# A cross-attention and mixture-of-experts block on one core: four differences moved, two PSUM banks read by other engines, one broadcast in two halves

## The chip, the cores and the metric

The kernel runs on one core of a Trainium2 chip. The metric is the device time of one execution in microseconds (us). Before the change it was 457.9 us, the median of three runs (457.46 to 458.61).

The engines are named as the profile names them: PE (TensorE, matrix products, with PEld for the loading of its stationary operand), DVE (VectorE), ACT (ScalarE), POOL (GpSimd) and SP (the queue that issues most transfers). Each engine works through its own list of instructions in order.

## The reference

Eight sequences of 512 tokens with 256 features (x) each have a context of 64 rows and a condition vector. All is float32.

```python
nx = layer_norm(x, ln_gamma, ln_beta)                    # (8, 512, 256)
k, v = context @ Wk, context @ Wv                        # (8, 64, 256)
scores = einsum('bth,bph->btp', nx @ Wq, k) * 256 ** -0.5
evidence = softmax(scores) @ v
combined = concatenate([nx, evidence, anchor], axis=-1)  # 768 features
router_probs = softmax(combined @ router_W + router_b)   # 3 experts
h = silu(einsum('btc,ecr->bter', combined, e_w1) + e_b1) # 512 features per expert
expert_out = einsum('bter,erh->bteh', h, e_w2) + e_b2
routed = sum(expert_out * router_probs[..., None], axis=-2)
g = sigmoid(silu(combined @ gate_w1 + gate_b1) @ gate_w2 + gate_b2)
return x + g * (routed @ out_w + out_b)
```

Two rearrangements matter below. The evidence times the middle rows of an expert's first weight is computed as softmax(scores) times (v W), so that the kernel needs the products of v and W once for each sequence. And the router's probabilities weigh h ahead of the second layer, so that each row of h is multiplied by a number that belongs to the token and the expert.

## The kernel before

**Pairs.** The eight sequences are worked on in four pairs, j = 0 to 3. A pair goes through three stages: `gate_layer` (first layer of the gate), `half_layers` (first layers of the three experts, a table of slots that fixes the order of products and of the steps of the other engines) and `outputs` (second layers, gate, and the results' way out). Much of what pair j + 1 needs ahead of its gate layer is put into `outputs` of pair j, at points with names: "begin", "gate", "P1", "P8", "P5", "P6", "P2", "P7", "P3", "P4", in this order. The dictionaries `between` and `within` hold what is run at each point of `outputs` and of `gate_layer`. The whole body stands under a schedule written out by hand: each engine executes its instructions in the order in which the program issues them.

**Products of two sequences at once.** Blocks are multiplied by a scheme with seven products in place of eight (as Strassen's): sums and differences of blocks go in, and three banks of PSUM, called u, y and z, gather the results, so that a bank is read in the middle of a sequence of products, and the next product adds to what it holds. A product that comes after such a read has to wait for the engine that reads.

**The late products.** For the last two pairs (j = 2 and 3, `JS` is 2) the products of v and W are made by this scheme too, in two parts: part 0 holds the columns of the first two experts (512 columns to a product), part 1 those of the third expert (256 columns). `block_columns` names the blocks of W and where their differences go: in part 0 t1 lies in `ow_sb`, t2 in `mr` and t4 in a tile of its own; in part 1 t1 and t2 lie in the two halves of `ow_sb` and t4 in `mr`. `late_difference(part, n)`, n = 0 to 3, makes one of the four differences on DVE (line L885 of the profile). `late_product(part, n, ps)` makes product n, and `late_values` returns four steps, `first` to `fourth`, with the products and the reads of the banks between them: ACT copies (`nc.scalar.copy`, lines L911, L917, L923 and L928) and DVE additions (`plus`, L906).

Part 0 is run inside `outputs` of pair 1: `first` at "P5", `second` and `third` at "P6", to either side of the scores, `fourth` at "P7". The step that `third` returns, the DVE addition, is run after the exponents (`late.pop()()`). Part 1 is run inside `gate_layer` of pair 2: after the products 1, 5, 6 and 7 of the gate. There `third` and its addition are run together. The four differences that part 1 reads, `late_difference(1, n)`, are issued at "P3" of pair 1's `outputs`, after the third expert sum (`finish`, lines L1431 to L1433 on DVE and L1434 on POOL) and ahead of `turn_weights` (L743, L745).

`fourth` starts with product 4 into u, followed by product 3 into z.

**The router's weights.** `spread_probabilities` stores the probabilities of a pair, transposed, into a small tile `pd` in DRAM (four rows: two sequences times two halves of the tokens; four transfers, L800) and loads it, spread over all 128 partitions, into `pb` (one transfer, L804). Both are issued from POOL's queue. `weigh_chunk` (L1022) multiplies h by the part of `pb` that belongs to its sequence (`S["pb", j][:, i, ...]`), and `bias_sum` (L1406, L1411) reads it too. The order of these multiplications on DVE follows the slots' tables; in pair 0 it begins with three of the first sequence (i = 0), then one of the second; in the later pairs with one of the first, then additions, then one of the second.

Each transfer has a semaphore, and the engines that read its tile wait for it.

Of the kernel before, what the change touches and what calls it, by code (L numbers as in the profile page):

```python
# [16 lines left out]
def kernel(  # L17
# [51 lines left out]
    nc = tc.nc  # L69
    P = 128  # L70
# [29 lines left out]
    def bank(i, name):  # L100
        ps = psum.tile([P, 512], F32, tag=f"b{i}", name=name)
        bank_of[ps.name] = i
        return ps

    def spares(*banks):
        spare[:] = banks
# [469 lines left out]
    S = {}  # L576
# [216 lines left out]
    def spread_probabilities(j):  # L793

        n = E * NJ
        prT = work.tile([P, TB], F32, tag="prT", name=f"prT_{j}", bufs=1)
        nc.vector.transpose(prT, pr)
        pd = dram.tile([len(SIDES), E * NH], F32, tag="pd", name=f"pd_{j}")
        for q, (i, h) in enumerate(SIDES):
            nc.gpsimd.dma_start(  # L800
                pd[q].rearrange("(n c) -> n c", c=TB), prT[q * TB : q * TB + n, :]
            )
        S["pb", j] = work.tile([P, 2, 2, E, NH], F32, tag="pb", name=f"pb_{j}", bufs=1)
        nc.gpsimd.dma_start(  # L804
            S["pb", j].rearrange("p i h e t -> p (i h) (e t)"), pd.partition_broadcast(P)
        )

    def by_side(flat):
        return flat.rearrange("p (h t) -> p h t", h=2)
# [51 lines left out]
    def block_columns(part):  # L861

        if part not in late_v:
            if part == 0:
                c0, n = 0, RH
                t4 = const.tile([P, RH], F32, tag="late_t4", name="late_t4")
                ts = ow_sb.rearrange("p k n -> p (k n)"), mr[:, :, : B // 2, :], t4
            else:
                c0, n = 2 * RH, RH // 2
                ts = ow_sb[:, 0, :], ow_sb[:, 1, :], mr[:, 0, : B // 2, :].rearrange("p b c -> p (b c)")  # L870
            w = [
                [w1[:, KH + k, c0 + i * n : c0 + (i + 1) * n] for i in range(2)] for k in range(KH)
            ]
            late_v[part] = w, ts
        return late_v[part]

    def like(a, b):
        return a.rearrange("p (k n) -> p k n", k=KH) if len(b.shape) > 2 else a
# [9 lines left out]
    def late_product(part, n, ps, start=False):  # L888

        ((b11, b12), (b21, b22)), ts = block_columns(part)  # L890
        t1, t2, t4 = (t.rearrange("p k b c -> p k (b c)") if len(t.shape) > 3 else t for t in ts)
        rhs = {1: b11, 2: b21, 3: b22, 4: t4, 5: t1, 6: t2, 7: b12}[n]
        product(like(ps, rhs), block_rows(n), rhs, start)

    def late_homes(part):
        (c0, n) = (0, RH) if part == 0 else (2 * RH, RH // 2)
        first, second = S["vw", JS], w1[:, KH, :]
        return [a[:, c0 + i * n : c0 + (i + 1) * n] for a in (first, second) for i in range(2)]

    def late_values(part, banks):  # L900

        n = RH if part == 0 else RH // 2
        u, y, z = (bank(i, f"ps_late_{m}")[:, :n] for i, m in zip(banks, "uyz"))

        def plus(dst, ps):
            nc.vector.tensor_tensor(dst, dst, ps, ALU.add)  # L906

        def first():
            c11 = late_homes(part)[0]
            late_product(part, 1, u, True)  # L910
            nc.scalar.copy(c11, u)  # L911
            late_product(part, 2, y, True)
            plus(c11, y)

        def second():
            late_product(part, 6, u)
            nc.scalar.copy(late_homes(part)[1], u)  # L917

        def third():
            c22 = late_homes(part)[3]  # L920
            late_product(part, 7, u)
            late_product(part, 5, z, True)
            nc.scalar.copy(c22, z)  # L923
            return lambda: plus(c22, u)

        def fourth():
            late_product(part, 4, u)
            nc.scalar.copy(late_homes(part)[2], u)  # L928
            late_product(part, 3, z)
            plus(late_homes(part)[1], z)  # L930
            for g in (0, 1) if part == 0 else (2,):
                value_differences(JS, g)

        return first, second, third, fourth

    GROUPS = (NE // 2, *range(NE // 2))
# [4 lines left out]
    def product(ps, lhsT, rhs, start=False):  # L941

        return nc.tensor.matmul(ps, lhsT, rhs, start=start, stop=True, skip_group_check=not start)  # L943
# [587 lines left out]
    with tc.manual_schedule(engines=None):  # L1531
# [85 lines left out]
        for j in range(NP):  # L1617


            within, between = {}, {}  # L1620

            def put(where, n, step, *args):
                where.setdefault(n, []).append(lambda: step(*args))

            spares(7, 5)
            if j == 0:
                spares(4, 5, 1)
                copies = []

                def value_product(g):  # L1630
                    value_weights(0, g, lambda *args: copies.append(args), False)

                def copy_values():
                    nc.scalar.copy(*copies.pop(0))

                put(within, 1, value_product, 0)
                put(within, 1, begin_softmax)
                put(within, 5, copy_values)
                put(within, 6, load_table, AF.Silu)
                put(within, 3, value_product, 1)  # L1640
                put(within, 3, copy_values)
                put(within, "sums", end_softmax)
                put(within, 7, value_product, 2)
                put(within, 7, copy_values)
                put(within, 7, end_setup)
            elif j < JS:
                put(within, 3, value_weights, j, 1, nc.scalar.copy, False)
            elif j == JS:
                first, second, third, fourth = late_values(1, (6, 5, 7))
                put(within, 1, first)  # L1650
                put(within, 5, second)
                put(within, 6, lambda third=third: third()())
                put(within, 7, fourth)
            if j + 1 < NP:
                b0, b1 = 2 * j + 2, 2 * j + 3
                if j + 2 < NP:
                    put(between, "begin", load_x, b0 + 2)
                    put(between, "begin", load_x, b1 + 2)
                put(between, "begin", transpose_blocks, b0)
                put(between, "gate", regroup_x, b1)  # L1660
                put(between, "begin", value_weights, j + 1, E)
                put(between, "begin", store_router_rows, j + 1)
                put(between, "begin", spread_router_rows, j + 1)
                put(between, "P8", transpose_blocks, b1)
                if j + 1 == JS:
                    put(between, "P6", lambda: late[1]())
                put(between, "P6", scores, j + 1)
                if j + 1 == JS:
                    put(between, "P6", lambda: late.append(late[2]()))
                put(between, "P6", exponents, j + 1)  # L1670
                if j + 1 == JS:
                    put(between, "P6", lambda: late.pop()())
                put(between, "P6", combine_x, j + 1, nc.gpsimd)
                if j + 1 < JS:
                    put(between, "P6", value_weights, j + 1, 2)
                elif j + 1 == JS:

                    def late_start():
                        late[:] = late_values(0, (0, 2, 4))

                    put(between, "P1", late_start)
                    put(between, "P5", lambda: late[0]())
                    for n in range(4):
                        put(between, "P3", late_difference, 1, n)
                put(between, "P7", softmax, j + 1)
                if j + 1 < JS:
                    put(between, "P7", value_weights, j + 1, 0)
                elif j + 1 > JS:
                    put(between, "P7", value_differences, j + 1, 0)
                    put(between, "P3", value_differences, j + 1, 1)  # L1690
                put(between, "P7", evidence_logits, j + 1)
                put(between, "P7", router_logits, j + 1)
                if j + 1 == JS:
                    put(between, "P7", lambda: late[3]())
                put(between, "P3", turn_weights, j + 1)
                put(between, "P3", router_exp, j + 1)
            gate_layer(j, within)
            half_layers(j)
            outputs(j, between)
# [34 lines left out]
```

## Time and profile before

| | |
|---|---|
| median of the runs | 457.9 us |
| time of the profiled execution | 458.82 us |
| its span | 456.8 us |
| PE busy | 450.8 us, 1,801 matmuls |
| DVE busy | 363.6 us, 698 instructions |
| ACT busy | 214.5 us, 378 instructions |
| POOL busy | 95.2 us, 153 instructions |
| chain of waits, by engine | PE 87%, DVE 6%, DMA 3% |
| pb: KB each, issues | 1,536 KB, 4 |
| pb: from issue to landing | 6.5 to 8.3 us, median 7.2 |
| DVE idle until pb has landed | 6.6 us in two waits, the longer 5.1 |

The profile is of one execution. Its span runs from the first to the last instruction on the engines; the execution's own time is 2.0 us longer. A matmul's record is longer than its share of the engine, since matmuls are pipelined: a row of the timeline with "x2" and 1.02 us is two matmuls of 512 columns, and the next one starts 0.86 us after the first. So whether PE stands still is read from the starts of its matmuls. A weight load (PEld) is issued ahead of its matmul, and part of its wait is hidden. In rows of a timeline the columns are the start and the duration in us, the engine, the line, the operation, the tiles written and read, and in brackets the time that the engine was idle before and what ended it.

Four pairs mean four passes with nearly the same rows: pair 0 to about 100 us (its first part holds the set-up, its end the preparation of the second layers), pair 1 from there to 250, pair 2 to 355, pair 3 to the end, each `outputs` with the next pair's preparation in it.

### The profile page before, as it was taken

To read this page: it belongs to the slowest core of one execution; us is meant where nothing else is said; L and a number is where in the kernel's file an instruction comes from. 1 tells how busy PE (TensorE), PEld (TensorE's weight loads), DVE (VectorE), ACT (ScalarE), POOL (GpSimd) and SP (SyncE) were. 2 spreads that over 40 slices of the span, in tenths; PEclk is the share of its full clock that TensorE was granted. 3 is DMA by queue.
4 is the path that set the end of the run, shared out by engine and by line. 5 is a ranking of instruction groups with operands and counts; after the bars stand their busy time and mean duration, and the time that the engine had idled before them with its cause. 6 is when DMAs were issued, how large, how long until landed. Compare 5 with 4: busy or idle time off the path is not lost.

```text
span 456.8 us, 5532 instructions
## 1 busy us (share of the span) xinstructions
PE 450.8 (99%) x1801; PEld 220.0 (48%) x1801; DVE 363.6 (80%) x698; ACT 214.5 (47%) x378; POOL 95.2 (21%) x153
## 2 busy tenths in 40 slices
PE   9999999999999999999999999999999999999996
PEld 7554445664444444444444444444444445654445
DVE  2878989949698799769769999767979937677983
ACT  2545864564501675466240377558430356558000
POOL 5466600252431200001431220000252310000010
PEclk9999999999999999999999999999999999999999
DMA  8984672364012377202002238401202282000004
GB/s 263 384 174 103 101 242 37 59 126 51 3 23 47 88 197 137 65 0 47 7 11 35 43 144 165 67 0 19 35 0 47 41 201 36 1 0 0 1 17 76
DMA packets 119380, 35.32 MB, mean 77 GB/s; under 512 B 106012, under 2 KB 116312, under 8 KB 118840
## 3 DMA queue, kind: packets, MB, share of 16 engines
q1 hardware_dynamic: 115344, 27.02, 28.9%
q0 software_dynamic: 2080, 7.16, 4.6%
q10 hardware_dynamic: 1928, 0.80, 0.6%
q8 instruction: 14, 0.23, 0.2%
q14 instruction: 14, 0.11, 0.1%
HBM read 27.56 MB, written 7.39 MB: 77 GB/s over the span
## 4 chain that ended last, share of the span: by engine, by line
PE 87%; DVE 6%; DMA 3%; POOL 1%; issue 1%; ACT 0%; ACTq 0%; DVEq 0%; POOLq 0%
PE ps_u L943 39%; PE ps_z L943 18%; PE ps_y L943 13%; PE ps_gu L943 3%; PE ps_vw L822 3%; PE ps_w2o L547 2%; DMA pb<-pd 2%; PE ps_s L691 2%; PE ps_gz L943 2%; PE ps_tokens L943 1%; DVE h L1401 1%; DMA scr_w<-in_L_xcond_Wk_dram 1%; PE ps_v L356 1%; PE ps_late_u L943 1%; PE ps_m L356 1%; PE ps_gy L943 1%
## 5 line engine op out<-in xcount | busy, mean ns | idle before, releaser
L943 PE MATMUL ps_u<-nxT,w 64*128 64x512 f32 (+1 forms) x208 | 96.9, 591 | 0.0
L1022 DVE TENSOR_TENSOR h<-h,pb 128x512 f32<-128x512 f32 x96 | 62.6, 684 | 17.1 <-ACT h L979 10.4
L943 PE MATMUL ps_u<-h,w2o 128*128 128x512 f32 x144 | 63.9, 593 | 0.0
L979 ACT ACTIVATE h<-h,abias 128x512 f32<-128x512 f32 x72 | 49.1, 717 | 31.3 <-DVE h L985 31.2
L943 PE MATMUL ps_y<-nxT,w 64*128 64x512 f32 (+1 forms) x104 | 51.7, 590 | 0.0
L943 PE MATMUL ps_z<-nxT,ws 64*128 64x512 f32 (+1 forms) x104 | 51.5, 591 | 0.0
L943 PE MATMUL ps_z<-T,ws 64*128 64x512 f32 (+1 forms) x104 | 51.5, 590 | 0.0
L943 PEld LDWEIGHTS ps_u<-nxT,w 64*128 64x128 f32 (+1 forms) x208 | 37.4, 187 | 25.4 <-issue 22.1
L943 PE MATMUL ps_u<-T,ws 64*128 64x512 f32 (+1 forms) x104 | 49.4, 590 | 0.0
L943 PE MATMUL ps_u<-T,w 64*128 64x512 f32 x112 | 48.5, 590 | 0.0
L943 PEld LDWEIGHTS ps_u<-h,w2o 128*128 128x128 f32 x144 | 27.3, 190 | 32.9 <-issue 32.3
L943 PE MATMUL ps_z<-h,w2s 128*128 128x512 f32 x96 | 42.5, 592 | 0.0
L943 PE MATMUL ps_z<-wT,vw 64*128 64x512 f32 x78 | 39.2, 590 | 0.0
L988 ACT COPY h<-ps_u 128x512 f32<-128x512 f32 x48 | 27.7, 580 | 21.5 <-PE ps_u L943 21.4
L1434 POOL TENSOR_TENSOR yb<-yb,xb 128x512 f32<-128x512 f32 x14 | 20.8, 1483 | 69.9 <-DVE yb L1433 56.8
L1401 DVE TENSOR_TENSOR h<-h,h 128x1024 f32<-128x1024 f32 x24 | 30.9, 1342 | 0.0
L943 PEld LDWEIGHTS ps_z<-h,w2s 128*128 128x128 f32 x96 | 18.2, 190 | 23.0 <-issue 22.0
L943 PEld LDWEIGHTS ps_y<-nxT,w 64*128 64x128 f32 (+1 forms) x104 | 19.4, 187 | 12.2 <-issue 12.2
L943 PEld LDWEIGHTS ps_z<-T,ws 64*128 64x128 f32 (+1 forms) x104 | 19.2, 187 | 12.1 <-issue 10.9
L943 PEld LDWEIGHTS ps_z<-nxT,ws 64*128 64x128 f32 (+1 forms) x104 | 19.0, 187 | 12.0 <-issue 9.2
L943 PEld LDWEIGHTS ps_u<-T,ws 64*128 64x128 f32 (+1 forms) x104 | 18.3, 187 | 12.8 <-issue 11.9
L943 PEld LDWEIGHTS ps_u<-T,w 64*128 64x128 f32 x112 | 18.6, 187 | 12.2 <-issue 11.5
(271 smaller groups left out, 847.1 us busy)
## 6 DMA issues: line engine op xcount, KB each, us to landing
pb<-pd POOLq DMA_DIRECT2D x4, 1536.0 KB, 7.2
xb<-in_x_dram SPq DMA_DIRECT2D x64, 64.0 KB, 2.4
out_dram<-yb SPq DMA_DIRECT2D x56, 64.0 KB, 1.9
x<-in_x_dram SPq DMA_DIRECT2D x24, 128.0 KB, 2.8
xd<-x SPq DMA_DIRECT2D x24, 128.0 KB, 2.6
xg<-xd SPq DMA_DIRECT2D x48, 64.0 KB, 2.3
w<-in_L_xcond_e_w_dram SPq DMA_DIRECT2D x4, 512.0 KB, 6.9
scr_wa<-in_L_xcond_e_w_dram SPq DMA_DIRECT2D x3, 512.0 KB, 9.4
```

The lines of the kernel that those rows point to most:

```text
L356: nc.tensor.matmul(ps, w_sb[:, k, m * P : (m + 1) * P], src[:, k, :], start=(k == 0), stop=(k == KH - 1))
L547: nc.tensor.matmul(ps[:, d * H : (d + 1) * H], w2["T"][u % 2][:, c : c + P], ow_sb[:, k, :], start=(k == 0), stop=(k == KH - 1),)
L691: nc.tensor.matmul(ps[side(i, h), g * NH : (g + 1) * NH], mr[:, k, 2 * j + i, g * TB : (g + 1) * TB], S["nxT", 2 * j + i][:, k, h * NH : ( ...
L822: nc.tensor.matmul(ps, vT[:, k, j * 2 * CT : (j + 1) * 2 * CT], w1[:, KH + k, n0:n1], start=(k == 0), stop=(k == KH - 1),)
L943: return nc.tensor.matmul(ps, lhsT, rhs, start=start, stop=True, skip_group_check=not start)
L979: nc.scalar.activation(h, h if src is None else src, AF.Silu, bias=abias[:, c, 2 * j + i : 2 * j + i + 1])
L988: nc.scalar.copy(chunk(n, i, d), part)
L1022: nc.vector.tensor_tensor(h, h, S["pb", j][:, i, :, 2 * q // RC, :], ALU.mult)
L1401: nc.vector.tensor_tensor(d, p, m, ALU.subtract)
L1434: nc.gpsimd.tensor_tensor(yb, yb, S["xb", 2 * j + row][:, i, :], ALU.add)
```

## The change

Three places are edited.

1. `spread_probabilities` loads `pb` by two transfers, one for each sequence of the pair (two rows of `pd` each). Each waits for the two stores into its own rows.
2. `third` in `late_values` (used by both parts): ACT copies the bank u right after product 7, and DVE adds the bank z, where ACT copied z after product 5, and DVE added u.
3. The four `late_difference(1, n)` are issued at "P6" of pair 1's `outputs`, behind the addition of part 0's `third`, and no longer at "P3".

```diff
@@ spread_probabilities @@
-        nc.gpsimd.dma_start(
-            S["pb", j].rearrange("p i h e t -> p (i h) (e t)"), pd.partition_broadcast(P)
-        )
+        for i in range(2):
+            nc.gpsimd.dma_start(
+                S["pb", j][:, i].rearrange("p h e t -> p h (e t)"),
+                pd[2 * i : 2 * i + 2].partition_broadcast(P),
+            )
@@ late_values @@
         def third():
             c22 = late_homes(part)[3]
             late_product(part, 7, u)
+            nc.scalar.copy(c22, u)
             late_product(part, 5, z, True)
-            nc.scalar.copy(c22, z)
-            return lambda: plus(c22, u)
+            return lambda: plus(c22, z)
@@ the loop over the pairs @@
                 put(between, "P6", exponents, j + 1)
                 if j + 1 == JS:
                     put(between, "P6", lambda: late.pop()())
+                    for n in range(4):
+                        put(between, "P6", late_difference, 1, n)
                 put(between, "P6", combine_x, j + 1, nc.gpsimd)
...
                     put(between, "P1", late_start)
                     put(between, "P5", lambda: late[0]())
-                    for n in range(4):
-                        put(between, "P3", late_difference, 1, n)
```

In the changed kernel's lists the products on PE, the copies on ACT and the operations on DVE keep their number and, but for the four differences on DVE, their order. What differs is the waits: product 4 of either part waits for ACT where it waited for DVE, product 3 for DVE where it waited for ACT, product 6 of part 1 for ACT alone. POOL issues four transfers more in all.

## The prediction

> **What bounds the kernel now.** First the page: TensorE is busy almost all the time, and its granted clock stands at the top digit in all forty slices.
>
> ```profile
> PE 450.8 (99%) x1801; PEld 220.0 (48%) x1801; DVE 363.6 (80%) x698; ACT 214.5 (47%) x378; POOL 95.2 (21%) x153
> ```
>
> So no edit that leaves the matmuls alone can win more than the stretches in which TensorE stands still, and it wins those only where it moves what TensorE waits for. I therefore read the waits of the weight loads, the chain of waits at the places the diff touches, and then the timeline there. In the waits (who <- whom: total us, times, longest) three groups matter:
>
> ```profile
> PEld ps_u L943 <- DVE h L985: 4.8, 9, 1.2
> ...
> PEld ps_late_u L943 <- DVE w L906: 1.8, 1, 1.8
> PEld ps_late_u L943 <- ACT vw L911: 0.9, 1, 0.9
> ```
>
> A weight load runs ahead of its matmul, so these are not yet stalls. A stall shows in the starts of the matmuls: without one, full 128-column products of 512 columns follow each other every 0.43 us (half that at 256 columns; a 64-row product runs beside its partner, so a pair also takes 0.43). I count what starts late against this pace.
>
> At the start of pair 2 (TensorE, start and us):
>
> ```profile
> 252.32 1.02 PE L943 MATMUL ps_z<-T,ws 128*128 128x512 f32 x2
> 253.40 0.67 PE L943 MATMUL ps_late_u<-ow_sb,vT 128*128 128x256 f32 x2
> ...
> 257.35 1.02 PE L943 MATMUL ps_u<-nxT,w 128*128 128x512 f32 x2
> 259.31 0.70 PE L943 MATMUL ps_late_u<-mr,vT 128*128 128x256 f32 x2 [0.94 <-DVE w L906]
> ```
>
> 252.32 + 2 x 0.43 = 253.18, so the first starts 0.22 us late, and its pair takes 0.08 too long (the restart): 0.30. The second is due at 258.21 and starts at 259.31: 1.10, plus 0.11 of restart: 1.21. VectorE at that time:
>
> ```profile
> 230.15 0.68 DVE L906 TENSOR_TENSOR w<-w,ps_late_u 128x512 f32<-128x512 f32 x1
> 233.63 0.69 DVE L1431 TENSOR_TENSOR r<-r,ps_y 128x512 f32<-128x512 f32 x1 [2.81 <-PE ps_y L943]
> ...
> 251.46 0.38 DVE L885 TENSOR_TENSOR ow_sb<-w 128x256 f32<-128x256 f32 x1
> 251.88 1.38 DVE L885 TENSOR_TENSOR ow_sb<-w,ow_sb 128x256 f32<-128x256 f32 x1
> ...
> 258.85 0.41 DVE L906 TENSOR_TENSOR w<-w,ps_late_u 128x256 f32<-128x256 f32 x1
> ```
>
> It runs without a pause from 233.63 to 259.85. The four differences (L885, 251.46 to 253.85: 2.39 us) lie inside that run, ahead of the addition (258.85 to 259.26) whose end releases the late product at 259.31. Before 233.63 it is idle for 2.81 us.
>
> In pair 0 the chain of waits (start, us) goes through the broadcast of the router's weights:
>
> ```profile
> 56.70 7.84 DMA pb<-pd
> 64.57 2.50 DVE h L1022 x4
> 67.07 0.61 DVE h L985
> 67.72 0.69 PE ps_u L943
> ```
>
> VectorE ends its last step at 63.10 and idles 1.47 us for pb. From 64.57 to 91 it never rests again, and TensorE stalls behind it: at 67.72 (due 67.21) 0.62 with the restart; between 76.41 and 79.55, where six steps take 3.14 instead of 2.57, 0.57; at 80.44, 0.13. Sum 1.32. In pair 3 VectorE idles 5.14 us for pb (371.93 to 377.07); TensorE feels 0.20 of it (378.41, due 378.31, and 0.10 restart). Pairs 1 and 2 have no wait on pb.
>
> Together the diff's places hold 1.32 + 0.20 + 0.30 + 1.21 = 3.03 us of stalled TensorE.
>
> **The differences, and which engine reads which bank.** Added and removed instructions on TensorE, VectorE and ScalarE: none; only order and operands change.
>
> *Part 0 (third() in pair 1, near 227).* ScalarE's copy now follows product 7 (done about 227.5) and not product 5 (its copy started at 228.48), so the copy, the logits copy behind it and the exponentials come about 1 us earlier; VectorE's addition then waits for product 5, done about 228.4, and ends near 229.9 instead of 230.83. TensorE has no stall from 229 to 253, so this wins nothing itself. Then the four differences: their nearest rows are 0.38, 0.41 and 0.41, starting 0.33 to 0.42 apart, so about 1.5 us; at worst the 2.39 of their old place. They end between 231.4 and 232.3 (from 230.83: at most 233.2), ahead of 233.63, in VectorE's idle time: price 0. If that cover were gone, the row-sum chain after 233.63 would start up to 2.4 us later, and be where it is today by 253.85.
>
> *Pair 2.* VectorE's queue is 2.39 us shorter from 251.46 on: the two additions L906 move from 258.54 to about 256.2, the second then waiting for product 5 (done about 256.6), so ending near 257. The product at 253.40 no longer waits for the difference (its bank was read by ScalarE at 252.52): its 0.30 goes. The product at 259.31 now waits for ScalarE's copy of u. That copy was at 256.69 behind product 5; behind product 7 it ends near 256.4. It is due at 257.9: no stall. Product 3, next, waits for VectorE's addition near 257 and is due at 258.3. So 1.51 goes. Margin: 1.3 us.
>
> What could eat it is GpSimd working beside VectorE:
>
> ```profile
> 251.61 1.36 POOL L1434 TENSOR_TENSOR yb<-yb,xb 128x512 f32<-128x512 f32 x1 [7.95 <-DVE yb L1433]
> ```
>
> It covers the difference that took 1.38 instead of 0.41. After the move a transpose (L743) stands there; in pair 3 one ran beside the same GpSimd line (356.40 to 357.91) in 0.71 us, its ordinary 0.71. The Trainium skill (SBUF — State Buffer, "SBUF: two separate sides") says that a VectorE operation with two SBUF inputs and a GpSimd operation exclude each other for a whole instruction. By it the differences could lose up to one GpSimd operation in their new place too, where the last of GpSimd's four (228.60 to 229.87) ends as they begin. Their dearest row, 2.39 us, fits in any case, as shown above. I take 1.51; bounds 0.3 (only the first stall goes) and 1.51.
>
> **The broadcast in two.** One issue (0.56 us on GpSimd) becomes two, eight instead of four in all; GpSimd has nothing urgent behind them (a memset of 0.12). The first half waits for two of the four small stores only. Those are issued 0.5 us apart, so it can go about 1 us earlier (55.7); the second goes at about 56.7 as today. The trace's DMA records show what the 7.84 us hold: nothing until 57.97, then 128 packets of 12,288 bytes over 16 engines, eight each, median 0.545 us, the slowest engine ending at 64.15. Half as many bytes per packet: the first half lands between 60 and 61.5 (four old packets' worth, or the slow engine's half), if time goes by bytes. If it goes by packets, it lands like today's whole less 1 us: 63.5. VectorE wants it at 63.10. The second half is wanted only at 64.9 (three products of 0.6 later); by bytes it is there by 64.6, by packets (2 x 8 x 0.545 from 57.0) at about 66. VectorE is ahead of today until the second half comes later than 64.57 + 1.8 = 66.4.
>
> By bytes VectorE gains 1.47 in pair 0 and keeps it, since the sums it reads next are all finished earlier than that; TensorE's 1.32 goes (upper end 1.55, with a stall of 0.23 at 87.78 that a transpose on VectorE ends). By packets VectorE resumes its fourth product at 66 and not 66.4: some 0.4. Nearest row: packets of 1,024 bytes in the same records take 0.046 to 0.07, so bytes decide; I take 1.32. In pair 3 the half is there before ScalarE's silu (373.72) lets VectorE go: 0.20.
>
> The Trainium skill (DMA: Bandwidth & Descriptors, "Anatomy of one DMA") speaks against the split: about 2 us fixed per DMA and bytes at 436 GB/s. By it two halves one after the other would be an estimated 7.6 us against 5.6 for the whole; from 55.7 that is 63.3 for the second.
>
> **Sum.** 1.51 + 1.32 + 0.20 = 3.03 us. The profiled execution took 458.82 (span 456.8 and 2.0 around it), 0.9 over the median of the runs, 457.9; its stalls count the same in both. 457.9 - 3.0 = **454.9**. Its own range: 454.2 (with the 0.23 and scatter) to 455.8.
>
> **Rivals.**
> - *Only the late products win.* Both halves land together, or packets decide: 457.9 - 1.5 = 456.4. For it: one queue, the same 16 engines. Against: the second half starts behind the first. 0.10.
> - *The wait moves to product 3.* It now needs VectorE's addition, where ScalarE's copy was enough. If VectorE arrives as late as today (259.3), product 3, due 258.3, stalls 1.0: of 1.51 remains 0.5, total 455.9. For it: the addition is still last of a long run. Against: 2.39 us less ahead of it. 0.12.
> - *Nothing shows:* the next late engine takes the stalls back, 457.6 to 457.9. Against: from 264 to 309 no product starts late. 0.07.
> - *Slower: the second half comes late.* If a half-size packet takes as long as a whole one on the slow engine too (6.2 us for eight, so 12.4 for sixteen, from 57.0), it lands at 69.8: 3.4 us past 66.4, and pair 3 likewise (11.7 from 369.1 against 380.07) 1.5. 457.9 - 1.5 + 3.4 + 1.5 = 461.3. It decides from a landing at about 68. Against: the 1,024-byte rows. 0.05.
>
> **How the numbers follow.** All three terms: 0.66. Range 454.0 to 456.8: it takes in the first two rivals and leaves out the last two. About 0.3% (1.4 us) is what a measurement of this kernel can tell from no change, so faster means under 456.5: 0.66 + 0.12 + half of the first rival, less a little for scatter, 0.80. Same: 0.14. Slower: 0.06.
>
> **What would show it.** Right: no wait of ps_late_u on VectorE; L885 near 230; two pb issues per pair, the first landed by 62 in pair 0, and L1022 starting at 63.1. Wrong: VectorE idle before the fourth L1022 of pair 0 past 66.4; a late product 3; the stalls at 78 and 80 still there.

## The result, and the profile after

The changed kernel takes 455.19 us in the median of six runs (454.99 to 455.48), against 457.81 for six runs of the kernel before beside them: a ratio of 0.994 (0.9928 to 0.9953), 2.6 us less. The profiled execution took 454.99 us, its span 453.2.

The page's busy times and the chain of waits by engine:

```profile
PE 448.6 (99%) x1801; PEld 214.4 (47%) x1801; DVE 363.8 (80%) x698; ACT 214.5 (47%) x378; POOL 96.8 (21%) x157
...
PE 99%; DVE 0%; issue 0%
```

The counts are the old ones but for POOL, which has the four further transfers. The chain that was 87% PE, 6% DVE and 3% DMA is now PE alone: for nearly the whole span it never leaves TensorE for another engine.

In the waits of the weight loads (who <- whom: total us, times, longest), these are all that the late products have left; "issue" is no other engine, and the one wait on ACT is hidden, as its matmul starts on time:

```profile
PEld ps_late_u L945 <- issue: 3.5, 14, 0.4
...
PEld ps_late_z L945 <- issue: 1.0, 4, 0.2
...
PEld ps_late_y L945 <- issue: 0.5, 2, 0.2
...
PEld ps_late_u L945 <- ACT vw L913: 0.2, 1, 0.2
```

The start of pair 2, timeline of TensorE:

```profile
250.50 1.02 PE L945 MATMUL ps_z<-T,ws 128*128 128x512 f32 x2
251.35 0.59 PE L945 MATMUL ps_late_u<-ow_sb,vT 128*128 128x256 f32 x2
...
255.22 1.02 PE L945 MATMUL ps_u<-nxT,w 128*128 128x512 f32 x2
256.08 0.59 PE L945 MATMUL ps_late_u<-mr,vT 128*128 128x256 f32 x2
256.51 0.59 PE L945 MATMUL ps_late_z<-w,vT 128*128 128x256 f32 x2
```

Product 6 is due at 250.50 + 0.86 = 251.36, product 4 at 255.22 + 0.86 = 256.08, product 3 0.43 behind it. All three are on time; before, the first was 0.22 late and the second 1.10, each with 0.1 of restart.

The same kernel's timeline of VectorE, at the new place of the differences and at the old one:

```profile
227.99 0.67 DVE L908 TENSOR_TENSOR w<-w,ps_late_z 128x512 f32<-128x512 f32 x1
228.59 0.41 DVE L887 TENSOR_TENSOR ow_sb<-w 128x256 f32<-128x256 f32 x1
...
229.72 0.42 DVE L887 TENSOR_TENSOR mr<-w,ow_sb 128x256 f32<-128x256 f32 x1
231.81 0.69 DVE L1433 TENSOR_TENSOR r<-r,ps_y 128x512 f32<-128x512 f32 x1 [1.67 <-PE ps_y L945]
...
249.64 0.67 DVE L743 STREAM_TRANSPOSE wT<-w 128x512 f32<-128x512 f32 x1
...
254.63 0.42 DVE L908 TENSOR_TENSOR w<-w,ps_late_z 128x256 f32<-128x256 f32 x1
```

The four differences run from 228.59 to 230.14, 1.55 us and none of them stretched, and VectorE still idles 1.67 us behind them. At the old place the transposes follow at once, and the addition that product 3 waits for ends at 255.05, 1.46 us before that product starts.

The router's weights in pair 0, on POOL's timeline and then on VectorE's:

```profile
55.64 1.17 POOL L805 DMA_DIRECT2D pb<-pd  x2 [0.97 <-DMA pd<-prT]
```

```profile
62.73 0.08 DVE L642 DVE_READ_ACCUMULATOR junk<-x,gg 128x1 f32 x1
62.73 2.49 DVE L1024 TENSOR_TENSOR h<-h,pb 128x512 f32<-128x512 f32 x4
```

The first half is issued at 55.64 (before: the whole at 56.70), and VectorE goes from its last step straight into the multiplications; the 1.47 us for pb are gone. On TensorE the product that started 0.51 late before is due at 66.50 + 0.43 = 66.93:

```profile
66.93 0.59 PE L945 MATMUL ps_u<-wT,vw 64*128 64x512 f32 x1
```

TensorE starts nothing late between 34 and 82. In pair 3 the multiplication starts at 370.41 behind ACT's silu, where it stood behind pb until 377.07. The view of the tile pb counts the issues and their landing, and lists no wait of VectorE on it any more:

```profile
L805 POOL DMA_DIRECT2D pb<-pd x8: 537/551/563, 55.6 to 365.8; - x8
...
DMA to landing us min/median/max: 4.1/4.9/7.5
```

Counted by the starts of the matmuls, the two profiles differ by 1.54 us of stalls in pair 0 (the 0.23 at 87.78 among them), 1.50 in pair 2 and 0.21 in pair 3: 3.25. That is more than the 2.6 between the medians. The experiments say why.

### The profile page after: what moved, and what is told of

It is laid out like the page before. It is cut to its first block, busy times and chain, and to the rows that moved or that the text cites. A ratio compares the mean times of both kernels' runs of the same rounds, so it can differ in the third digit from the quotient of the medians.

```text
span 453.2 us, 5537 instructions
## 1 busy us (share of the span) xinstructions
PE 448.6 (99%) x1801; PEld 214.4 (47%) x1801; DVE 363.8 (80%) x698; ACT 214.5 (47%) x378; POOL 96.8 (21%) x157
## 4 chain that ended last, share of the span: by engine, by line
PE 99%; DVE 0%; issue 0%
PE ps_u L945 45%; PE ps_z L945 20%; PE ps_y L945 14%; PE ps_gu L945 3%; PE ps_vw L824 3%; PE ps_w2o L547 2%; PE ps_s L691 2%; PE ps_gz L945 2%; PE ps_tokens L945 1%; PE ps_late_u L945 1%; PE ps_wake L316 1%; PE ps_v L356 1%; PE ps_m L356 1%; PE ps_gy L945 1%; PE ps_late_z L945 1%; PE pt_x L619 0%
## 5 line engine op out<-in xcount | busy, mean ns | idle before, releaser
L1436 POOL TENSOR_TENSOR yb<-yb,xb 128x512 f32<-128x512 f32 x14 | 20.6, 1474 | 67.6 <-DVE yb L1435 54.5
L1403 DVE TENSOR_TENSOR h<-h,h 128x1024 f32<-128x1024 f32 x24 | 30.9, 1342 | 0.0
```

What stands on the lines that cost most here:

```text
L1403: nc.vector.tensor_tensor(d, p, m, ALU.subtract)
L1436: nc.gpsimd.tensor_tensor(yb, yb, S["xb", 2 * j + row][:, i, :], ALU.add)
```

## The experiments

Ten kernels ran, in three groups, each beside runs of the kernel before: 457.83 us (22 runs) for the first three, 458.01 (23) for the next four, 457.90 (7) for the last three. `x_after` ran in the first group alone. So a difference between kernels of two groups also holds the up to 0.2 us between the runs of before, and where one is used below, the difference of the last column stands beside it.

| run | what it holds | median us (range) | ratio (95%) | against before |
|---|---|---|---|---|
| x_after | the change | 455.23 (454.94–455.58) | 0.9945 (0.9932–0.9959) | -2.60 |
| x_halves | two transfers alone | 456.85 (456.61–457.39) | 0.9979 (0.997–0.9987) | -0.98 |
| x_late | banks and differences, one transfer | 456.34 (455.52–457.17) | 0.9971 (0.9961–0.9981) | -1.49 |
| x_banks | banks alone | 457.51 (456.73–458.24) | 0.9989 (0.998–0.9999) | -0.50 |
| x_moved | differences alone | 456.31 (456.04–456.36) | 0.9966 (0.9953–0.9979) | -1.70 |
| x_reversed | the change, second sequence's half sent first | 456.49 (456.14–457.00) | 0.9966 (0.9955–0.9978) | -1.52 |
| x_fill12 | the change, 12 further operations on VectorE | 457.37 (457.19–457.87) | 0.9986 (0.9977–0.9995) | -0.64 |
| x_stores | the change, small stores in the order 3, 4, 1, 2 | 455.13 (454.94–455.56) | 0.9946 (0.9931–0.9962) | -2.77 |
| x_noswap | two transfers and differences, banks as before | 455.13 (454.86–455.35) | 0.9945 (0.9929–0.996) | -2.77 |
| x_fill6 | as x_fill12, with 6 | 454.88 (454.81–455.48) | 0.9939 (0.9921–0.9957) | -3.02 |

**The change in its two parts.** `x_after` is the changed kernel itself. `x_halves` takes the first hunk of the diff alone; `x_late` takes the other two.

```diff
@@ x_halves: spread_probabilities, nothing else @@
-        nc.gpsimd.dma_start(
-            S["pb", j].rearrange("p i h e t -> p (i h) (e t)"), pd.partition_broadcast(P)
-        )
+        for i in range(2):
+            nc.gpsimd.dma_start(
+                S["pb", j][:, i].rearrange("p h e t -> p h (e t)"),
+                pd[2 * i : 2 * i + 2].partition_broadcast(P),
+            )
```

> The changed kernel once more, beside the two halves of the change, on one chip. My theory: the stalls taken away add up, 1.32 (with 0.23 more: 1.55) in pair 0, 1.51 in pair 2, 0.20 in pair 3, so 3.0 to 3.3 us less than before. Rival: one of the stalls is not there in every execution of the kernel before, as the single profile of it was a long one; then the gain over many executions is nearer to the 2.6 us of the medians.

> Only the broadcast in two. My theory: 1.5 to 1.75 us less than before, no late product on TensorE in pairs 0 and 3, and the two stalls of pair 2 (0.30 and 1.21 us) still there. Rival (the wait for pb is short in most executions): under 1 us.

> Only the late products: banks swapped and differences moved, one broadcast. My theory: 1.5 us less than before, stalls of pairs 0 and 3 as before (1.3 to 1.55, and 0.2). Rival (the wait moves to product 3): 0.5 to 1.0 us.

The parts add up: 0.98 + 1.49 = 2.47, against 2.60 together. Each takes away its own stalls and leaves the other's. Pair 2 of x_halves, on TensorE's timeline:

```profile
250.45 1.02 PE L945 MATMUL ps_z<-T,ws 128*128 128x512 f32 x2
251.52 0.67 PE L945 MATMUL ps_late_u<-ow_sb,vT 128*128 128x256 f32 x2
...
255.47 1.02 PE L945 MATMUL ps_u<-nxT,w 128*128 128x512 f32 x2
257.42 0.70 PE L945 MATMUL ps_late_u<-mr,vT 128*128 128x256 f32 x2 [0.93 <-DVE w L908]
```

251.52 for 251.31 and 257.42 for 256.33: both stalls are there as before, 0.2 and 1.1, though pair 0 has none. So the stalls of the late products move with pair 2 and do not depend on what pair 0 lost; what they are bound to is taken apart next. x_late has no stall there, and keeps a wait on pb in pair 0, on VectorE's timeline:

```profile
63.59 2.50 DVE L1022 TENSOR_TENSOR h<-h,pb 128x512 f32<-128x512 f32 x4 [0.45 <-DMA pb<-pd]
```

That is 0.45, where the profile of before had 1.47 with the same single transfer. It is the first hint at the size that was wrong. The profile of x_halves also has a small stall that the others do not have (312.32, 0.31 late, released by ACT's copy at L1371). If it is there in most executions, the halves take away some 0.3 more than the 0.98; that is not shown.

**Banks and differences apart.** `x_banks` has the hunk of `third` alone, `x_moved` the one of the loop alone.

```diff
@@ x_banks: third, nothing else @@
+            nc.scalar.copy(c22, u)
             late_product(part, 5, z, True)
-            nc.scalar.copy(c22, z)
-            return lambda: plus(c22, u)
+            return lambda: plus(c22, z)
@@ x_moved: the loop over the pairs, nothing else @@
                     put(between, "P6", lambda: late.pop()())
+                    for n in range(4):
+                        put(between, "P6", late_difference, 1, n)
...
-                    for n in range(4):
-                        put(between, "P3", late_difference, 1, n)
```

> Only the two banks swapped; the differences stay where they were, one broadcast. Theory A (VectorE's queue is what is late, and the four differences make it so): product 4 of part 1 is let go by ScalarE, but product 3 behind it waits for VectorE's addition, which still ends near 259.3; the stall at product 6 (0.30) stays, and of the 1.21 some 0.4 is won. Theory B (the swap is what counts): about 1.2 us less than before.

> Only the four differences moved; the banks are read as before, one broadcast. Theory A: VectorE reaches its addition about 2.2 us earlier, product 4 is not held up, both stalls of pair 2 go: 1.5 us less than before, as much as with the swap. Theory B: only product 6's 0.30 goes, as product 4 still waits for VectorE.

x_moved wins all of the part (1.70; x_late 1.49, their ranges overlap), and its products of pair 2 are all on time. Product 4, due at 256.60 + 0.86 = 257.46, on TensorE's timeline:

```profile
256.60 1.02 PE L943 MATMUL ps_u<-nxT,w 128*128 128x512 f32 x2
257.45 0.59 PE L943 MATMUL ps_late_u<-mr,vT 128*128 128x256 f32 x2
```

x_banks wins 0.50, with an interval that nearly reaches no change; its starts say the same, 0.43 less of stall in pair 2 than before. Its pair 2, on TensorE's timeline, and the addition on VectorE's:

```profile
252.50 0.67 PE L943 MATMUL ps_late_u<-ow_sb,vT 128*128 128x256 f32 x2
...
257.30 0.59 PE L943 MATMUL ps_late_u<-mr,vT 128*128 128x256 f32 x2
258.40 0.70 PE L943 MATMUL ps_late_z<-w,vT 128*128 128x256 f32 x2 [0.50 <-DVE w L906]
```

```profile
257.94 0.41 DVE L906 TENSOR_TENSOR w<-w,ps_late_z 128x256 f32<-128x256 f32 x1
```

Product 4 is on time, since ScalarE reads its bank. Product 3, due at 257.73, now waits for VectorE's addition, which ends at 258.35: 0.67 late. This is the rival "the wait moves to product 3" as it was described; it decides where the differences stay in front of that addition, and not where they go.

**Does the swap of banks do anything beside the move?** `x_noswap` is the change without the hunk of `third`.

```diff
@@ x_noswap: the change, with third as before @@
-            nc.scalar.copy(c22, u)
             late_product(part, 5, z, True)
-            return lambda: plus(c22, z)
+            nc.scalar.copy(c22, z)
+            return lambda: plus(c22, u)
```

> The changed kernel with the two banks read as before (ScalarE copies z, VectorE adds u): broadcast in two, differences moved. Theory A (moving the differences does all that is won in pair 2): the time of the changed kernel, no late product in pair 2. Theory B (the swap has its own part when the other two edits are there): 0.3 to 1.2 us longer.

It takes 455.13, x_after 455.23; x_stores, which has the swap and ran in the same group, takes 455.13 too. Product 4 of x_noswap waits for VectorE again, and that wait is over in time (TensorE):

```profile
255.09 1.02 PE L945 MATMUL ps_u<-nxT,w 128*128 128x512 f32 x2
255.94 0.59 PE L945 MATMUL ps_late_u<-mr,vT 128*128 128x256 f32 x2
```

Due at 255.95 and there at 255.94. With the differences out of the way, which engine reads which bank makes no difference to the time that these runs can tell.

**How much room VectorE has.** `x_fill12` and `x_fill6` issue further subtractions of the differences' size behind them. They write a tile that nothing reads.

```diff
@@ x_fill12; x_fill6 with range(6) @@
+    def filler():
+        fill_t = work.tile([P, 2 * P], F32, tag="pv", name="fill_t", bufs=1)
+        some = ws[:, S1, :2, :].rearrange("p q c -> p (q c)")
+        nc.vector.tensor_tensor(fill_t, some, some, ALU.subtract)
...
                     for n in range(4):
                         put(between, "P6", late_difference, 1, n)
+                    for n in range(12):
+                        put(between, "P6", filler)
```

> The changed kernel with twelve more subtractions of 128x256 on VectorE right behind the four moved ones; they write a tile that nobody reads. They take about 0.43 us each, 5.2 in all. Theory A (the moved differences cost nothing because of 1.67 us that VectorE is idle there, and because the addition that product 3 waits for ends 1.46 us early): 3.1 us of them are free, and product 3 stalls for the other 2.1. Theory B (VectorE's time there is on the path all along): 5.2 us more than the changed kernel; theory C (VectorE has room after that too): nothing.

> The changed kernel with six more subtractions of 128x256 on VectorE behind the four moved ones, about 2.7 us. Theory A (there is room for some 3.1 to 3.5 us, of which the twelve used 5.5 and lost the rest): nothing is lost, no product of pair 2 starts late. Theory B (VectorE's time there counts in proportion, as 2.1 of 5.5 were lost with twelve): 1.0 us longer.

Twelve cost 457.37 - 455.23 = 2.14 us (1.96 by the last column) and six nothing. The size is as forecast, but the place is another. VectorE's timeline of x_fill12 first, then TensorE's:

```profile
229.90 5.46 DVE L848 TENSOR_TENSOR fill_t<-ws 128x256 f32<-128x256 f32 x12
235.28 0.68 DVE L1438 TENSOR_TENSOR r<-r,ps_y 128x512 f32<-128x512 f32 x1
...
250.96 0.69 DVE L1438 TENSOR_TENSOR r<-r,ps_z 128x512 f32<-128x512 f32 x1
```

```profile
249.48 0.59 PE L950 MATMUL ps_late_u<-w,vT 128*128 128x256 f32 x2
251.70 0.70 PE L950 MATMUL ps_late_y<-w,vT 128*128 128x256 f32 x2 [1.63 <-DVE r L1438]
...
257.82 0.59 PE L950 MATMUL ps_late_u<-mr,vT 128*128 128x256 f32 x2
258.53 0.70 PE L950 MATMUL ps_late_z<-w,vT 128*128 128x256 f32 x2
```

The late product that stalls most is product 2 of part 1, the first into y: 249.48 + 0.43 = 249.91 is when it is due, and it starts 1.79 late. Its bank held a sum of the output that VectorE reads at 250.96 (L1438), a read that the prediction had not counted. The changed kernel's rows give the sum. There this read (247.50 to 248.19) ended 1.44 ahead of the product before (249.63) and 1.87 ahead of product 2 (250.06). With twelve fillers it ends at 251.65, 2.17 behind the product before (249.48), so VectorE is 3.61 late. Of these 1.87 are free, and 1.74 are left; product 2 starts 1.79 late, with 0.11 of restart. Product 3 had 1.46: 3.61 - 1.90 - 1.46 = 0.25 more, measured 0.28 and 0.10. So the room ahead of product 3 is the smaller of the two, and the total, 3.61 less 1.46, is as forecast; but product 2 comes first and takes most of it. The profile has a further 0.20 in pair 3 (a product at 364.31), whose cause is open. Six fillers (2.71) make VectorE 0.85 late, counted in the same way, less than either room.

**What of the two transfers pays: the earlier issue, or the half that comes first?** `x_reversed` sends the half of the second sequence first, which VectorE wants last. `x_stores` leaves the halves in order and stores the two rows of the first sequence last, so that its half can't go earlier.

```diff
@@ x_reversed @@
-        for i in range(2):
+        for i in (1, 0):
@@ x_stores @@
-        for q, (i, h) in enumerate(SIDES):
+        for q in (2, 3, 0, 1):
```

> The changed kernel with the two halves of the broadcast in the other order: the second sequence's half first. It waits for the third and fourth store, so nothing is issued earlier than the one broadcast was, and the half that VectorE wants first is the last to land. Theory A (what pays is that the half wanted first is issued 1 us earlier and is half as long): VectorE waits for it in pair 0 again, till 64 to 64.6, and 1.0 to 1.3 us of pair 0's gain is lost; in pair 3 nothing, as VectorE has 3 us to spare there. Theory B (two transfers move the bytes faster than one, whatever their order): both have landed by 63, and the time is that of the changed kernel.

> The changed kernel with the four small stores in the order third, fourth, first, second: the half that VectorE wants first is still sent first, but it now waits for the last store, so it goes at about 56.4 us, when the one broadcast went. Theory A (what pays is that the half wanted first stands ahead of the other and is half as long): it lands by 62, VectorE does not wait in pair 0, and the time is that of the changed kernel. Theory B (what pays is being issued up to 1 us earlier): VectorE waits 0.4 to 1 us, and the time is 0.4 to 1 us longer.

x_reversed gives back 456.49 - 455.23 = 1.26 us (1.08 by the last column). VectorE's timeline of it, then TensorE's:

```profile
64.26 2.50 DVE L1024 TENSOR_TENSOR h<-h,pb 128x512 f32<-128x512 f32 x4 [1.32 <-DMA pb<-pd]
```

```profile
67.41 0.69 PE L945 MATMUL ps_u<-wT,vw 64*128 64x512 f32 x1 [0.18 <-DVE h L987]
```

The wait is there again with two transfers, as long as with one, and the stalls behind it too: 1.38 us in pair 0. x_stores takes 455.13, as the change. Its POOL and VectorE:

```profile
56.24 1.10 POOL L805 DMA_DIRECT2D pb<-pd  x2 [1.61 <-DMA pd<-prT]
```

```profile
62.68 2.49 DVE L1024 TENSOR_TENSOR h<-h,pb 128x512 f32<-128x512 f32 x4
```

Issued 0.6 us later than in the change's profile, and no wait in pair 0: by the records of the transfers its last packet, of both halves, ends at 62.83, after VectorE has begun. In the profile of x_after the first half also went late, at 56.22, and the last packet ends at 63.43; VectorE begins at 62.81, without a wait. In pair 3 of x_stores VectorE waits 2.20 for pb, and TensorE starts nothing late by it. So it is the order, the half wanted first coming first, that pays. The earlier issue is not needed.

**Why the halves win 0.9 to 1.1 and not 1.5.** Four profiles have the transfer in one piece. By the records its packets are under way for

| | packets, first to last | VectorE waits | PE stalls, pair 0 | pair 3 |
|---|---|---|---|---|
| before | 57.97 to 64.15 (6.18) | 1.47 | 1.54 | 0.21 |
| x_late | 58.01 to 63.27 (5.26) | 0.45 | 0.50 | 0.44 |
| x_banks | 57.52 to 63.14 (5.62) | 1.01 | 1.06 | 0 |
| x_moved | 57.61 to 63.69 (6.08) | 1.38 | 1.43 | 0 |

The mean is 1.13 in pair 0 and 0.16 in pair 3, together 1.29; the profile that the prediction read, with 1.75, holds the longest wait of the four. That the medians show 0.9 to 1.1 and not 1.29 is left open: four executions are few.

## Why the prediction was right, and where a number was off

The time on record was 454.9 us; 455.19 was measured. The account was right where time was won. One size was off, and one wait that costs nothing was read wrongly.

- *The late products, 1.51.* Right in size and place: 1.49 (x_late), 1.70 (x_moved), and 456.85 - 455.23 = 1.62 where the halves are there too. The differences went into VectorE's idle time as laid out, 1.55 us long (the sum had about 1.5), and 1.67 idle was left. Of two reasons given for the gain only one was needed: the queue 2.39 us shorter ahead of the additions. The other, that product 4 then waits for ScalarE, does nothing for the time (x_noswap).
- *Part 0, third().* The sum had VectorE's addition wait for product 5 and end about 0.9 us earlier. The copy did move: VectorE's step behind it (L707) starts at 226.56 against 229.25, 0.86 earlier when the 1.83 is taken off by which TensorE runs ahead by then. But the negation of the row maximum (L717), 0.17 in before, takes 0.70 (227.38 to 228.08) beside GpSimd's last addition of L682 (226.78 to 228.05), and the addition waits for it and ends 0.34 earlier (228.66 against 230.83). This loss was not in the sum. The differences still ended 1.67 us before VectorE's next sum, so nothing hung on it.
- *GpSimd beside VectorE.* The difference that took 1.38 beside L1434 takes 0.42 at the new place, where GpSimd rests from 228.05 to 234.04. GpSimd's addition at the old place (249.79, 1.27) now lies beside the transposes, of which the first takes 0.67, and at 254.46 beside an addition that reads PSUM (0.42): neither is stretched. The Trainium skill (SBUF — State Buffer, "SBUF: two separate sides") names the pairs that exclude each other, a VectorE operation with two SBUF inputs (against a GpSimd operation that reads SBUF) or in a two-port mode against a GpSimd operation; these rows agree with it.
- *The margin, 1.3 us at product 3.* 1.46 by the rows of the change, and the smallest room that the runs show. What the prediction did not see is product 2, with 1.87: VectorE must first have read its bank, and with twelve fillers it takes most of the loss.
- *The broadcast, 1.32 in pair 0 and 0.20 in pair 3.* The mechanism held: half the bytes take half the time (median 0.460 to 0.545 us for 12,288 bytes in the profile of before, 0.234 to 0.244 for 6,144 in that of the change), the first half has landed at 59.96, where 60 to 61.5 was forecast, and the second is never late. **The term of the sum that was mis-sized is this one:** 1.52 were put in, 0.98 (x_halves), 1.11 (x_late to x_after) and 1.08 (x_moved to x_after; 0.90 by the last column) were measured. The step that failed is "its stalls count the same in both", the profiled execution and the median. The profile lay 0.9 us above the median, and part of that was this very wait, which varies from execution to execution (the table above). The stall hangs on when the last packet of one transfer lands, so one execution does not give its size. The 0.23 at 87.78, left out of the sum as an upper end, went too: the two profiles differ by 3.25, so without this omission the sum would have been farther off.
- *The earlier issue.* Counted as part of the mechanism; x_stores shows the order alone to be enough.
- *The second transfer's fixed time.* Both halves together are under way from 56.90 to 62.57 in the change's profile, 5.7 us, against 5.3 to 6.2 for the one transfer. The Trainium skill (DMA: Bandwidth & Descriptors, "Anatomy of one DMA") gives about 2 us fixed for each transfer; the runs here do not show it added for the second. From the first issue to the second landing it is 7.5 us (55.64 to 63.18), as the prediction's estimate from that page has it (7.6), but the one transfer takes 7.8 from issue to landing and not the 5.6 of the same estimate.
- *Rivals.* "Only the late products win" and "the second half comes late" fell with x_halves and the change's profile. "The wait moves to product 3" is real in x_banks and absent in the change. "Nothing shows" fell: the stalls went and none took their place.

What stays open: about 0.3 us of the difference between the two profiles lies ahead of 20 us, in the set-up, where the diff changes nothing; the twelve profiles leave the set-up from 0.15 us earlier to 0.48 later than that of the change, whatever the kernel. No run makes VectorE between 1.46 and 1.87 late, where product 3 should give way alone. And whether the wait for pb makes the scatter of the runs is not shown: the kernel before ranged over 2 us in 52 runs, but x_moved, with the same single transfer, over 0.3 in five.

## What to carry to other kernels

Work for later that stands in a queue ahead of what the bounding engine is about to need should go into an earlier idle gap of the same engine; which engine reads which bank then mattered nothing here, and alone it moved the wait by one product and won 0.5 of the 1.5 to 1.7. A transfer whose parts are wanted at different times can go in pieces, the first-wanted first: here it is the order that paid, and the pieces in the wrong order paid nothing. And a stall that ends with a transfer's landing should be sized from several executions, not from the one that was profiled.

## What the runs showed of the hardware that was not expected

- One and the same 1,536 KB transfer, at the same point of the program, was under way for 5.26 to 6.18 us, 0.9 us of spread, and VectorE's wait for it ranged from 0.45 to 1.47 (four profiles, pair 0).
- A GpSimd addition of 128x512 (L1436) took 2.15 at 234.04, beside the VectorE products of two SBUF tiles (L1403) that run from 233.89 to 238.42. At 240.56, where it started 0.04 ahead of VectorE's L736, also with two SBUF inputs, it took 1.27, and L736 took 1.78 where it had 0.69 at 25.50 with GpSimd at rest. In these rows the operation that came second is the longer one, on either engine.
- The negation of a row maximum on VectorE (L717, 128x8, in pair 1) took 0.17 in the four profiles where GpSimd rests beside it, and 0.69 or 0.70 in the eight where one of GpSimd's additions of L682 runs beside it.
- After each stall TensorE loses a further 0.1 us (the first pair's second product starts 0.53 instead of 0.43 behind the first), and about 0.2 where it changes from 128-row to 64-row products (256.51 to 257.04 and 257.57 in the change). This second loss stands in every pair of the change's profile.
